# Joining, scaling and the order of the closing norms in a graph-attention kernel

## The chip, the cores and the metric

The kernel runs on one core of a Trainium2 chip. The metric is device time in microseconds (us) of one execution. TensorE, VectorE, ScalarE, GpSimd and SyncE have a queue of instructions each and run them in order; they wait for each other with semaphores. In the profile they are called PE, DVE, ACT, POOL and SP. Nearly all plain copies between memory and the on-chip SBUF are issued by SyncE.

## The reference

There are 12,500 nodes with 128 features and 412,500 edges with 64 features, sorted by target.

```python
h = node_features @ Wn + bn                      # own row of each node
hmid = leaky_relu(concat(q[src], k[tgt], eh) @ A1 + b1)
scores = leaky_relu(hmid @ A2 + b2)
w = softmax(scores.mean(axis=-1), axis=0)        # over all edges
out = segment_sum(w[:, None] * v[tgt], src, num_segments=num_nodes)
y = h + out                                      # "joined"
n = gamma * (y - mean(y)) / sqrt(var(y) + EPS) + beta   # first norm
x = layernorm(x + n)                                    # second norm
```

The softmax runs over all edges, so its denominator is known only when the last edge's score is. Until then each node's sum is kept with a reference of its own; the last step multiplies each sum by one factor and adds the own row `h`. Then come two norms over the 128 features of each node.

## The kernel before, in words

The 128 partitions hold the nodes: partition `p` holds 98 nodes in a row ("blocks" 0 to 97). A first stage (`make`) computes a record for each edge and scatters the records into tables by block. A second stage (`sums_of`) goes over 294 units (six passes over pairs of blocks) and adds weighted values to each node's sum, which is stored in the table `atab`. This second stage takes nearly all of the time. It runs a schedule written out by hand: `do(step, fn, ...)` puts a function into a numbered step, and when the program is built, the functions of one step are emitted after each other in the order in which they were put in. Each engine's queue therefore has exactly this order.

The part that is changed is `closing` (L1333 onward), which begins while the last units are still at work. It has three stages.

- Beside the second stage, `rows_x`, `moved` and `put_x` add `beta` to the node features and store them in `xtab` (GpSimd, L1354), and `load_gamma` loads `gamma` into SBUF.
- When the last unit's maximum is known, `factors`, `whole`, `spread_z`, `over_z`, `lowered_all` and `scaled_all` compute `facs`, one factor for each block (`scaled_all`, L1397, is the last).
- Then the 98 blocks are finished in 14 groups of `NB` = 7 blocks. A group is `7 x 128 = 896` numbers on each partition.

For a group the steps before the change are these. `fetch` (SyncE, L1428) loads own rows `hs`, sums `part` and moved features `xs`, each 448 KB, into one buffer of the pool `rt` (six buffers). `joined` (VectorE, L1463, seven instructions) multiplies the sum by its factor and adds the own row. `spread` (VectorE, L1440 and L1441, seven pairs) computes mean and variance of each block; `root` (ScalarE, L1444) takes the square root; `scales` (VectorE, L1447 and L1448) computes the reciprocal and an offset; `normed` (ScalarE, L1455, seven instructions) applies both. `gained` multiplies by `gamma` (VectorE, L1469) and adds `xs` (GpSimd, L1470). Then `spread`, `root`, `scales` and `normed` follow a second time, and `leave` (SyncE, L1473) writes the group to the output.

The groups overlap as a hand-written pipeline. In its step `t` the queues get, in this order: `spread` of group `t`, `gained` of group `t - 1`, the second `spread` of group `t - 2`, the first `normed` of group `t`, `joined` of group `t + 1` and the second `normed` of group `t - 2`. A group is joined in the step before its first spread, and the last group's last work is in step 15.

Of the kernel before, what the change touches and what calls it, by code (L numbers as in the profile page):

```python
# [10 lines left out]
FP = mybir.dt.float32  # L11
# [3 lines left out]
AF = mybir.ActivationFunctionType  # L15
ALU = mybir.AluOpType
# [4 lines left out]
P = 128  # L21
D = 128
# [4 lines left out]
NB = 7  # L27
# [5 lines left out]
NP = 6  # L33
CUTS = 0, 0.1266, 0.2804, 0.4615, 0.6427, 0.8238, 1
TABS = 2
WIDTH = 14
# [3 lines left out]
WR = 260  # L40
# [335 lines left out]


def first_layer(nc, banks, pk, bias):

    W = pk[:, : 4 * D].rearrange("k (s d) -> k s d", s=4)  # L380
    A1s = pk[:, 4 * D : 7 * D].rearrange("k (s d) -> k s d", s=3)
    wT = pk[:, 7 * D : 9 * D].rearrange("k (s d) -> k s d", s=2)
    weT2, cols = pk[:, 9 * D : 9 * D + 2 * DE], pk[:, 9 * D + 2 * DE : 9 * D + 2 * DE + 3]

    pw = banks[0][:, : 2 * D].rearrange("p (s d) -> p s d", s=2)
    for s in (1, 0):
        nc.tensor.matmul(pw[:, s, :], wT[:, s, :], A1s[:, s, :], start=True, stop=True)
# [60 lines left out]
def sorted_path(  # L448
# [8 lines left out]
    nc = tc.nc  # L457
# [3 lines left out]
    NBK = nb + 1  # L461
# [13 lines left out]
    ident = const.tile([P, P], FP)  # L475
# [68 lines left out]
    ng = nb // NB  # L544
# [11 lines left out]
    rp = pool("rec", 6)  # L556
    pkvp = pool("pkv", 1, space=PSUM)
    pcp = pool("pcn", 1, space=PSUM)
# [11 lines left out]
    php = pool("ph", 2, space=PSUM)  # L570
    pscp = pool("psc", 1, space=PSUM)
# [12 lines left out]
    start = const.tile([1, G], I32)  # L584
# [79 lines left out]
    with tc.tile_pool(name="prep", bufs=1) as prep:  # L664
        bank = psmp.tile([P, 4 * P], FP, name="psm")
        banks = bank[:, : 2 * D], bank[:, 2 * D :], pscp.tile([P, 4 * P], FP, name="psc")
        pk, bias = load_weights(nc, prep, pack, rows_b)
        load_first()
        W, We_, bias = first_layer(nc, banks, pk, bias)
# [6 lines left out]
        for b in range(0, NB, 2):  # L676
            m = min(2, NB - b)
            at = nodes[b // 2][:, : 2 * D * m]
            for k in range(m):
# [40 lines left out]
    def spans():  # L720
# [24 lines left out]
        out=above, in_=above, compare_op=ALU.is_gt, fill=0.0, base=0,  # L745
# [8 lines left out]
    pcs = {}  # L754
# [232 lines left out]
    for p, t in enumerate(plan.tiles):  # L987
        wide = max(1, min(2, WIDTH // t))
# [347 lines left out]
    def closing(bp, do, s0, s1, s2):  # L1336

        gb = {}

        def wide(b):  # L1340
            return b.rearrange("p (o d) -> p o d", o=1).to_broadcast([P, NB, D])

        def three(b, k):
            return b[:, k * NB * D : (k + 1) * NB * D].rearrange("p (b d) -> p b d", d=D)
# [86 lines left out]
        def spread(st, y, k):  # L1431
            if k == 1:
                own = (oldp, "old") if st["bl"].start // NB % 2 else (scp, "part")
                st["sm"] = own[0].tile([P, 2, D], FP, name=own[1])
            sm = st["sm"][:, k - 1, :]
            st["mv", k] = mv = sm[:, : 2 * NB].rearrange("p (b s) -> p b s", s=2)
            st["rstd", k], st["off", k] = sm[:, 2 * NB : 3 * NB], sm[:, 3 * NB : 4 * NB]
            for j in range(NB):
                s6 = sm[:, 4 * NB + 6 * j : 4 * NB + 6 * j + 6]
                nc.vector.bn_stats(s6, st[y][:, j, :])  # L1440
                nc.vector.bn_aggr(mv[:, j, :], s6)  # L1441

        def root(st, k):
# [6 lines left out]
                op0=ALU.mult, op1=ALU.mult,  # L1450
            )

        def normed(st, to, y, k):
            for j in range(NB):
                nc.scalar.activation(  # L1455
                    st[to][:, j, :], st[y][:, j, :], AF.Identity, bias=st["off", k][:, j : j + 1],
                    scale=st["rstd", k][:, j : j + 1],
                )

        def joined(st):  # L1460
            for j in range(NB):
                b = st["bl"].start + j
                nc.vector.scalar_tensor_tensor(  # L1463
                    st["hs"][:, j, :], st["part"][:, j, :], gb["facs"][:, b : b + 1], st["hs"][:, j, :],
                    op0=ALU.mult, op1=ALU.add,
                )

        def gained(st):
            nc.vector.tensor_mul(st["n1"], st["n1"], wide(gb["gamma"]))  # L1469
            nc.gpsimd.tensor_add(st["n1"], st["n1"], st["xs"])  # L1470

        def leave(st):
            nc.sync.dma_start(out=out[:, st["bl"], :], in_=st["o"])  # L1473
# [236 lines left out]
```

## Time and profile before

| What | Value |
|---|---|
| Median of 3 runs | 5028.19 us (5021.88 to 5036.83) |
| The profiled execution's own time | 5024.54 us |
| Its span, from the first to the last instruction | 5022.8 us |
| Busy share of the span: PE, DVE, ACT, POOL | 83%, 79%, 65%, 67% |
| Last multiplication on TensorE ends at | about 4880.7 us |
| Last norm on ScalarE ends at | about 5014.6 us |

A row of the profile's timeline has the start in us, the duration in us, the engine, the line of the kernel, the operation, its output and inputs, the shape of the output and of the first input, and how many equal instructions were merged (`x7`). In brackets stands the engine's idle time ahead of it. The groups of instructions by line have `busy us in total, mean ns of one`, then the idle time before them. A row of the table of stretches has the stretch, its length, the busy time of each engine with its number of instructions, the granted TensorE clock (1.00 is full speed), the share in which the DMA engines were busy, and GB/s.

### The profile page before, as it was taken

To read this page: it belongs to the slowest core of one execution; us is meant where nothing else is said; L and a number is where in the kernel's file an instruction comes from. 1 tells how busy PE (TensorE), PEld (TensorE's weight loads), DVE (VectorE), ACT (ScalarE), POOL (GpSimd) and SP (SyncE) were. 2 spreads that over 40 slices of the span, in tenths; PEclk is the share of its full clock that TensorE was granted. 3 is DMA by queue.
4 is the path that set the end of the run, shared out by engine and by line. 5 is a ranking of instruction groups with operands and counts; after the bars stand their busy time and mean duration, and the time that the engine had idled before them with its cause. 6 is when DMAs were issued, how large, how long until landed. Compare 5 with 4: busy or idle time off the path is not lost.

```text
span 5022.8 us, 97600 instructions
## 1 busy us (share of the span) xinstructions
PE 4158.4 (83%) x32218; PEld 3108.6 (62%) x32676; DVE 3991.7 (79%) x10036; ACT 3267.8 (65%) x8495; POOL 3348.4 (67%) x3268
## 2 busy tenths in 40 slices
PE   4565578898888888799998898999899999899980
PEld 3333356666566666577776676676667777667760
DVE  7877576788777777688888888888888888677778
ACT  3433255666566666577777777777677777677876
POOL 5777777777777777777777777777777777410002
PEclk7777588899999999899999999999999999999995
DMA  7999799998899988899989888989899999788763
GB/s 262 314 318 344 255 328 333 343 312 300 274 324 324 329 301 289 275 318 318 313 308 311 302 315 311 309 307 313 301 306 314 315 324 318 265 287 283 262 224 141
DMA packets 614992, 1505.49 MB, mean 300 GB/s; under 512 B 103587, under 2 KB 328246, under 8 KB 612681
## 3 DMA queue, kind: packets, MB, share of 16 engines
q1 hardware_dynamic: 459433, 1069.47, 65.0%
q0 software_dynamic: 154752, 429.39, 22.7%
q8 instruction: 259, 4.24, 0.3%
q14 instruction: 260, 2.13, 0.1%
q10 hardware_dynamic: 288, 0.26, 0.0%
HBM read 929.49 MB, written 608.37 MB: 306 GB/s over the span
## 4 chain that ended last, share of the span: by engine, by line
DMA 37%; PE 24%; DVE 16%; POOL 9%; issue 6%; ACT 6%; SPq 1%; DVEq 0%; ACTq 0%; POOLq 0%
DMA rtab<-rec,idx 14%; DMA rt<-rtab 13%; POOL rtab L904 9%; PE psm L1268 6%; DMA row<-slT 4%; PE ph L1116 4%; PE pkv L881 3%; PE ph L1107 3%; DMA rowB<-row 3%; DVE hm L1131 2%; PE psc L1144 2%; PE pkv L875 2%; ACT rec L892 2%; PE psm L1177 2%; ACT ohw L1239 2%
## 5 line engine op out<-in xcount | busy, mean ns | idle before, releaser
L904 POOL DMA_INDIRECT rtab<-rec,idx x3224 | 3286.2, 1019 | 1042.0 <-issue 781.0
L892 ACT ACTIVATE rec<-pkv 128x1024 f32<-128x1024 f32 x806 | 819.9, 1017 | 863.5 <-PE pkv L881 475.4
L1239 ACT ACTIVATE ohw<-ohs,w 128x128 f32<-128x128 bf16 x3822 | 1258.7, 400 | 58.4 <-DVE ohs L1225 47.9
L1268 PE MATMUL psm<-rt,ohw 128*128 128x128 f32 x7644 | 1158.6, 294 | 10.7 <-ACT ohw L1239 10.6
L1268 PEld LDWEIGHTS psm<-rt,ohw 128*128 128x128 f32 x7644 | 997.5, 200 | 59.5 <-ACT ohw L1239 17.7
L1127 ACT ACTIVATE hm<-ph 128x512 f32<-128x512 f32 (+1 forms) x1078 | 581.7, 540 | 461.6 <-PE ph L1116 429.0
L1116 PE MATMUL ph<-ohT,qs 128*128 128x512 bf16 (+3 forms) x3658 | 718.1, 312 | 25.5 <-issue 2.6
L1131 DVE TENSOR_TENSOR hm<-ph,hm 128x512 f32<-128x512 f32 (+1 forms) x1078 | 668.5, 620 | 83.3 <-ACT hm L1127 81.9
L875 PE MATMUL pkv<-kvs,ohd 128*128 128x256 bf16 x3224 | 531.4, 292 | 204.0 <-ACT rec L892 189.7
L1107 PE MATMUL ph<-ident,rt 128*128 128x128 f32 x3822 | 629.3, 283 | 45.8 <-DVE hm L1131 43.4
L881 PE MATMUL pkv<-WeS,eat 64*128 64x128 f32 x6448 | 633.6, 320 | 0.0
L1096 DVE TENSOR_SCALAR ohT<-rowB,iotaP 128x512 bf16<-128x512 uint8 (+1 forms) x1078 | 518.4, 481 | 102.1 <-DMA rowB<-row 97.2
L881 PEld LDWEIGHTS pkv<-WeS,eat 64*128 64x128 f32 x6448 | 467.9, 205 | 191.8 <-issue 184.9
L875 PEld LDWEIGHTS <-ohd 128*128 128x128 bf16 x3224 | 316.2, 103 | 317.5 <-issue 224.5
L1107 PEld LDWEIGHTS ph<-ident,rt 128*128 128x128 f32 x3822 | 471.9, 152 | 64.1 <-DVE hm L1131 51.0
L1116 PEld LDWEIGHTS <-qs 128*128 128x128 bf16 x4116 | 396.8, 100 | 129.4 <-issue 4.8
L1225 DVE TENSOR_TENSOR ohs<-iotaE,sl 128x512 bf16<-128x512 bf16 (+1 forms) x1078 | 427.1, 396 | 48.4 <-ACT ohw L1239 46.8
L844 DVE TENSOR_TENSOR ats<-pc,oh 128x792 f32<-128x792 f32 x403 | 392.1, 973 | 82.1 <-PE pc L826 76.9
L1144 PE MATMUL psc<-hm,A2s 128*32 128x512 f32 (+3 forms) x2352 | 337.7, 538 | 80.1 <-DVE slT L1075 75.9
L1177 PE MATMUL psm<-headsum,z 128*128 128x4 f32 (+1 forms) x2156 | 287.9, 255 | 128.0 <-DVE part L1284 87.0
L855 DVE TENSOR_REDUCE pos<-ats 128x8 f32<-128x792 f32 x403 | 390.2, 968 | 4.2
L1177 PEld LDWEIGHTS psm<-headsum,z 128*128 128x128 f32 (+1 forms) x2156 | 280.9, 202 | 149.4 <-DVE part L1284 102.6
(161 smaller groups left out, 4080.2 us busy)
## 6 DMA issues: line engine op xcount, KB each, us to landing
rt<-rtab SPq DMA_DIRECT2D x196, 1820.0 KB
eat<-in_ea SPq DMA_DIRECT2D x201, 512.0 KB
rt<-rtab SPq DMA_DIRECT2D x49, 1560.0 KB
rt<-rtab SPq DMA_DIRECT2D x49, 1300.0 KB
qs<-qtab SPq DMA_DIRECT2D x294, 192.0 KB
rtab<-rec,idx POOLq DMA_INDIRECT x3224
dstb<-dtab SPq DMA_DIRECT2D x201, 256.0 KB
rtab<-empty SPq DMA_DIRECT2D x98, 520.0 KB
```

Of the source, the lines that this page charges most:

```text
L875: nc.tensor.matmul(pk[:, h, i, :], ohd[:, t * P : (t + 1) * P], kvs, start=(i == 0), stop=False,)
L881: nc.tensor.matmul(pk[:, h, i, :D], eat[h * DE : (h + 1) * DE, (j + i) * P : (j + i + 1) * P], WeS[h * DE : (h + 1) * DE, :], start=False, ...
L892: nc.scalar.activation(rec[:, :, :, : 2 * D], pk, AF.Copy)
L904: one_tile = nc.gpsimd.indirect_dma_start(out=rtab[p % TABS][:, :], out_offset=bass.IndirectOffsetOnAxis(ap=idxs[g][:, t : t + 1], axis=0) ...
L1096: nc.vector.tensor_scalar(st["oh"][k][:, : n * P], st["rowB"][:, t0 * P : (t0 + n) * P], iotaP, None, op0=ALU.is_equal,)
L1107: nc.tensor.matmul(ph[:, j * P : (j + 1) * P], st["rt"][:, t0 + j, :D], ident, is_transpose=True, start=(j == 0), stop=False,)
L1116: nc.tensor.matmul(ph[:, cols], st["qs"][:, j0 // t, s, :], oh[:, cols], start=False, stop=(s == 2 and j1 == t0 + n),)
L1127: nc.scalar.activation(hm, state[i]["ph", k][:, : n * P], AF.Copy, scale=SLOPE)
L1131: nc.vector.tensor_tensor(hm, ph[:, : n * P], hm, op=ALU.max)
L1177: nc.tensor.matmul(st["psS"][:, t0 + j : t0 + j + (nv - 1) * sw + 1 : sw], z[: 32 * nv, j * P : (j + 1) * P], headsum[: 32 * nv, :nv], sta ...
L1239: nc.scalar.activation(ohw[:, j, :], ohs[:, :, j], AF.Copy, scale=st["w"][:, t0 + j : t0 + j + 1])
L1268: nc.tensor.matmul(st["psS"][:, (1 + u) * P : (2 + u) * P], ohw[:, j, :], st["rt"][:, t0 + j, D : 2 * D], start=(k == 0), stop=(k == t - 1),)
```

## The change

Nothing outside `closing` does other work; the tile `pc` of the first stage is only allocated at the width of the others (512 numbers instead of 99), so that `closing` can use its buffer. In `closing`:

- `diagonals` is new: GpSimd multiplies the identity matrix by the factors of four pairs of blocks, which gives four 128 x 128 diagonal matrices (two neighbouring blocks share one, because they come from one unit and have the same factor).
- `joined` moves to TensorE: two multiplications by the identity bring the own rows into PSUM (512 and 384 columns), and seven multiplications by a diagonal add the scaled sums. Three sets of PSUM buffers are used in turn: `pkv`; two `ph`; `psc` and `pc`.
- The first `spread` and the first `normed` read PSUM; `normed` writes its result into a buffer of the pool `rec`, and the second norm is written in place and leaves from there.
- `gained` multiplies by `gamma` on GpSimd instead of VectorE.
- A group takes one step more, and the order within a step is another. `scales` of both norms stand in the middle of a `spread` of another group.

```diff
     def begin(p):
-        pcs[p] = pcp.tile([P, NBK], FP, name="pc")
+        pcs[p] = pcp.tile([P, 4 * P], FP, name="pc")[:, :NBK]
...
-            st["n1"], st["o"] = three(rt, 3), st["part"]
+        pairs = max(1, min(2, WIDTH // plan.tiles[NP - 1]))
+        def diagonals(st):
+            b0, b1 = st["bl"].start // pairs * pairs, st["bl"].stop
+            n = -(-(b1 - b0) // pairs)
+            rec = rp.tile([P, 2, 2, WR], FP, name="rec").rearrange("p a b w -> p (a b w)")
+            dg = rec[:, : n * P].rearrange("p (n d) -> p n d", n=n)
+            nc.gpsimd.tensor_tensor(
+                dg, ident.rearrange("p (o d) -> p o d", o=1).to_broadcast([P, n, P]),
+                gb["facs"][:, b0:b1:pairs].rearrange("p (n o) -> p n o", o=1)
+                .to_broadcast([P, n, P]),
+                op=ALU.mult,
+            )
+            st["dg"] = lambda b: dg[:, (b - b0) // pairs, :]
+        def joined(st):
+            g = st["bl"].start // NB
+            if g % 3 == 0:
+                pk = pkvp.tile([P, 2, 2, 2 * D], FP, name="pkv").rearrange("p h i w -> p h (i w)")
+                st["y"] = pk[:, 0, :], pk[:, 1, :]
+            elif g % 3 == 1:
+                st["y"] = [php.tile([P, 4 * P], FP, name="ph") for _ in range(2)]
+            else:
+                st["y"] = (
+                    pscp.tile([P, 4 * P], FP, name="psc"), pcp.tile([P, 4 * P], FP, name="pc")
+                )
+            for k, to in enumerate(st["y"]):
+                m = min(4, NB - 4 * k)
+                nc.tensor.matmul(
+                    to[:, : m * P], ident,
+                    st["hs"][:, 4 * k : 4 * k + m, :].rearrange("p b d -> p (b d)"),
+                    start=True, stop=False,
+                )
+                for j in range(m):
+                    nc.tensor.matmul(
+                        to[:, j * P : (j + 1) * P], st["dg"](st["bl"].start + 4 * k + j),
+                        st["part"][:, 4 * k + j, :], start=False, stop=(j == m - 1),
+                    )
...
-        def joined(st):
-            for j in range(NB):
-                b = st["bl"].start + j
-                nc.vector.scalar_tensor_tensor(
-                    st["hs"][:, j, :], st["part"][:, j, :], gb["facs"][:, b : b + 1], st["hs"][:, j, :],
-                    op0=ALU.mult, op1=ALU.add,
-                )
...
         def gained(st):
-            nc.vector.tensor_mul(st["n1"], st["n1"], wide(gb["gamma"]))
+            nc.gpsimd.tensor_mul(st["n1"], st["n1"], wide(gb["gamma"]))
             nc.gpsimd.tensor_add(st["n1"], st["n1"], st["xs"])
...
-        for t in range(-1, ng + 2):
+        for t in range(-4, ng + 3):
             s = first + t
-            at(s - 3, t + 1, fetch)
-            at(s, t, spread, "hs", 1)
-            at(s, t, root, 1)
-            at(s, t - 1, gained)
-            at(s, t - 2, spread, "n1", 2)
-            at(s, t - 2, root, 2)
-            at(s, t, scales, 1)
-            at(s, t, normed, "n1", "hs", 1)
-            at(s, t + 1, joined)
-            at(s, t - 2, scales, 2)
-            at(s, t - 2, normed, "o", "n1", 2)
-            at(s, t - 2, leave)
+            at(s, t + 4, fetch)
+            at(s, t + 2, diagonals)
+            at(s, t + 1, joined)
+            at(s, t - 1, normed, 1)
+            at(s, t, spread, 1, 0, 3)
+            at(s, t - 3, scales, 2)
+            at(s, t, spread, 1, 3, NB)
+            at(s, t, root, 1)
+            at(s, t - 3, normed, 2)
+            at(s, t - 3, leave)
+            at(s, t - 2, spread, 2, 0, 4)
+            at(s, t, scales, 1)
+            at(s, t - 2, spread, 2, 4, NB)
+            at(s, t - 2, root, 2)
+            at(s, t - 1, gained)
```

In the changed kernel the lines are: diagonals L1437, joined L1458 and L1464, spread L1483 and L1484, root L1487, scales L1490 and L1491, normed L1501, gained L1507 and L1508, leave L1511.

More of the change, by code (lines that the diff above doesn't have):

```diff
@@ L1428, in fetch, with of, spread @@
                 nc.sync.dma_start(out=st[name], in_=of[:, bl, :])
-            st["n1"], st["o"] = three(rt, 3), st["part"]
-        def spread(st, y, k):
+        pairs = max(1, min(2, WIDTH // plan.tiles[NP - 1]))
[34 more added lines that the diff above has]
+                    )
+        def of(st, k, j):
             if k == 1:
+                return st["y"][j // 4][:, j % 4 * P : (j % 4 + 1) * P]
+            return st["n1"][:, j, :]
+        def spread(st, k, j0, j1):
+            if k == 1 and j0 == 0:
                 own = (oldp, "old") if st["bl"].start // NB % 2 else (scp, "part")
@@ L1437, in spread @@
             st["rstd", k], st["off", k] = sm[:, 2 * NB : 3 * NB], sm[:, 3 * NB : 4 * NB]
-            for j in range(NB):
+            for j in range(j0, j1):
                 s6 = sm[:, 4 * NB + 6 * j : 4 * NB + 6 * j + 6]
-                nc.vector.bn_stats(s6, st[y][:, j, :])
+                nc.vector.bn_stats(s6, of(st, k, j))
                 nc.vector.bn_aggr(mv[:, j, :], s6)
@@ L1451, in scales, with normed @@
             )
-        def normed(st, to, y, k):
+        def normed(st, k):
+            if k == 1:
+                rec = rp.tile([P, 2, 2, WR], FP, name="rec").rearrange("p a b w -> p (a b w)")
+                st["n1"] = three(rec, 0)
             for j in range(NB):
                 nc.scalar.activation(
-                    st[to][:, j, :], st[y][:, j, :], AF.Identity, bias=st["off", k][:, j : j + 1],
-                    scale=st["rstd", k][:, j : j + 1],
-                )
-        def joined(st):
-            for j in range(NB):
-                b = st["bl"].start + j
-                nc.vector.scalar_tensor_tensor(
-                    st["hs"][:, j, :], st["part"][:, j, :], gb["facs"][:, b : b + 1], st["hs"][:, j, :],
-                    op0=ALU.mult, op1=ALU.add,
+                    st["n1"][:, j, :], of(st, k, j), AF.Identity,
+                    bias=st["off", k][:, j : j + 1], scale=st["rstd", k][:, j : j + 1],
                 )
         def gained(st):
-            nc.vector.tensor_mul(st["n1"], st["n1"], wide(gb["gamma"]))
+            nc.gpsimd.tensor_mul(st["n1"], st["n1"], wide(gb["gamma"]))
             nc.gpsimd.tensor_add(st["n1"], st["n1"], st["xs"])
         def leave(st):
-            nc.sync.dma_start(out=out[:, st["bl"], :], in_=st["o"])
+            nc.sync.dma_start(out=out[:, st["bl"], :], in_=st["n1"])
         groups = [dict(bl=slice(g * NB, (g + 1) * NB)) for g in range(ng)]
```

## The prediction

> **What bounds the kernel now.** I first read the table of stretches of the last 320 us, because only the closing changes: the queues keep their order up to the first diagonal.
>
> ```profile
> 4700.00:4862.00 162.00, 159.85 (x1229) 123.05 (x1245) 124.58 (x358) 132.01 (x390) 0.00 (x0) 1.00 0.69 232
> 4904.00:4994.00 90.00, 0.00 (x0) 0.00 (x0) 84.47 (x400) 59.17 (x160) 20.72 (x10) 0.50 0.48 175
> ```
>
> Up to 4862 PE is busy all the time. From 4904 to 4994 PE does nothing, DVE is busy for 84 of 90 us, ACT for 59, POOL for 21. The rest of the kernel can't gain; what is to be had lies here. Next, one period of the pipeline in the timeline of DVE, then the rows of ACT and POOL beside it:
>
> ```profile
> 4937.40 1.93 DVE L1463 SCALAR_TENSOR_TENSOR rt<-rt,hm 128x128 f32<-128x128 f32 x7
> 4939.25 0.19 DVE L1447 RECIPROCAL part<-part 128x7 f32<-128x7 f32 x1
> ...
> 4939.56 0.29 DVE L1440 BATCH_NORM_STATS2 old<-rt 128x6 f32<-128x128 f32 x1
> ...
> 4942.34 1.06 DVE L1469 TENSOR_TENSOR rt<-rt,eat 128x896 f32<-128x896 f32 x1
> 4943.32 0.29 DVE L1440 BATCH_NORM_STATS2 old<-rt 128x6 f32<-128x128 f32 x1
> ...
> 4946.10 0.17 DVE L1447 RECIPROCAL old<-old 128x7 f32<-128x7 f32 x1
> 4946.31 0.17 DVE L1448 SCALAR_TENSOR_TENSOR old<-old 128x7 f32<-128x7 f32 x1
> 4946.42 1.93 DVE L1463 SCALAR_TENSOR_TENSOR rt<-rt,hm 128x128 f32<-128x128 f32 x7
> ```
>
> ```profile
> 4937.20 0.30 ACT L1444 ACTIVATE part<-part,eps 128x7 f32<-128x7 f32 x1 [3.00 <-DVE part L1441]
> 4937.49 5.49 ACT L1455 ACTIVATE rt<-rt,part 128x128 f32<-128x128 f32 x14
> 4943.53 2.07 POOL L1470 TENSOR_TENSOR rt<-rt 128x896 f32<-128x896 f32 x1 [6.95 <-DVE rt L1469]
> ```
>
> DVE has no gap, so the period is the sum of its parts, from start to start: join 1.85, scales 0.31, spread 2.78, gamma 0.98, spread 2.78, scales 0.32: 9.02 us. ACT needs 5.49 + 2 x 0.29 = 6.07 and waits 3 us.
>
> **The change part by part.** Joins and gamma leave DVE: 9.02 - 1.85 - 0.98 = 6.19 us a step are left. That is the gain if nothing else ends later; so I ask of each other engine what its step becomes.
>
> ACT keeps its 14 norms and two roots, 6.07 us by the rows above; seven norms now read PSUM. The nearest rows:
>
> ```profile
> L1455 ACT ACTIVATE rt<-rt,part 128x128 f32<-128x128 f32 x98 | 38.5, 479 | 1.0 <-DVE part L1448 1.0
> L1159 ACT ACTIVATE z<-psc,b_c 96x512 f32<-96x512 f32 x8 | 5.3, 669 | 0.0
> L1159 ACT ACTIVATE z<-psc,b_c 32x256 f32<-32x256 f32 x8 | 3.7, 466 | 0.2
> ```
>
> The same function from PSUM costs 0.79 ns an element (203 ns for 256 elements more), so 0.365 us at 128 against 0.479 from SBUF. Seven take 2.74 us at the old spacing of 0.392, and 2.0 if all of that difference comes off the spacing. I keep both ends.
>
> The first spread reads PSUM. No row has it; L1284, with PSUM for one of its inputs, and L1463, with SBUF alone, cost the same:
>
> ```profile
> L1284 DVE SCALAR_TENSOR_TENSOR part<-old,by,psm 128x128 f32<-128x128 f32 x20 | 5.9, 338 | 0.0
> L1463 DVE SCALAR_TENSOR_TENSOR rt<-rt,hm 128x128 f32<-128x128 f32 x98 | 26.9, 345 | 0.0
> ```
>
> I take no difference; 0.05 us an instruction either way would be 0.35 a step.
>
> PE gets 896 identity and 896 diagonal columns a group. Warm and cold rows:
>
> ```profile
> 4650.90 0.89 PE psm L1268 x8
> 39.12 2.07 PE L1534 MATMUL ph<-hm,xt 128*128 128x256 f32 x4 [8.98 <-DMA xt<-in_xN]
> 25.00:50.00 25.00, 11.21 (x58) 7.45 (x59) 14.09 (x35) 3.94 (x6) 7.20 (x8) 0.63 0.76 220
> ```
>
> Eight records are four f32 multiplications of 128 columns (two records each): 0.22 us each at full clock, so 14 x 0.22 = 3.1 us a group. At the low clock two of 256 columns took 2.07: 14 x 0.52 = 7.2 us. A group can be joined as soon as the norm three groups earlier has read its PSUM, over a step before it is needed, so either fits in a step of 7.2 us or more. PE's price lies in the start, below. If its cover goes (a step below 7.2 with a cold PE), PE sets 7.2.
>
> The Trainium skill ("TensorE: Matmul & The Clock Gate", Part 1) says that the clock is halved by default and is released by some 3.4 us of sustained matmuls. The stretch with the clock at 0.63 and PE half busy agrees; by this rule the joins, bursts of 3 to 7 us, would run between the two prices, and the sum stays within mine.
>
> POOL gets a multiplication of 896 (L1354, an addition with a broadcast input, is the nearest) and the diagonals, 512 numbers:
>
> ```profile
> L1354 POOL TENSOR_TENSOR rec<-rec x14: 2085/2094/2272, 4366.8 to 4584.8; 128x896 f32<-128x896 f32 x14
> ```
>
> 2.09 for gamma, 2.07 for the addition; for the diagonals 512/896 x 2.07 = 1.18, with something fixed 1.25 (bounds: 1.2 and 2.1, a full row). Together 5.4 us with gaps of 0.1: below 6.19, but POOL is now nearly always busy. What that does to DVE is the crux:
>
> ```profile
> 4890.20 2.07 POOL L1470 TENSOR_TENSOR rt<-rt 128x896 f32<-128x896 f32 x1 [303.29 <-DVE old L1447]
> 4890.22 2.08 DVE L1448 SCALAR_TENSOR_TENSOR old<-old 128x7 f32<-128x7 f32 x1
> 4435.87 2.08 POOL L1354 TENSOR_TENSOR rec<-rec 128x896 f32<-128x896 f32 x1 [13.35 <-DMA rec<-in_beta]
> 4436.12 2.12 DVE L1096 TENSOR_SCALAR ohT<-rowB,iotaP 128x512 bf16<-128x512 uint8 x1
> 4943.74 0.26 DVE L1440 BATCH_NORM_STATS2 old<-rt 128x6 f32<-128x128 f32 x1
> ```
>
> The offset instruction of scales (0.17 us elsewhere) took 2.08 and ended with POOL's addition, which had begun 0.02 before. So did L1096, which reads one tensor: 2.12 us, to the end of the addition of 4435.87. Spreads are not held up (the one at 4943.74 runs within the POOL addition of 4943.53). Scales has one offset instruction, and there are two scales a step. Of its reciprocal (one tensor) no row tells; I take it to run like the spreads, and the other case is a rival.
>
> The Trainium skill ("SBUF — State Buffer", "Who interferes with whom") has this rule: a DVE instruction with two SBUF inputs and a GpSimd instruction that reads SBUF exclude each other, and the later one waits for the whole of the other. The trace agrees, with 2.08 us for the offset's two inputs. By the rule the reciprocal, with one, doesn't wait, and the sum is the one below; if it waited, that of rival 2.
>
> The steady step by hand, us from the start of DVE's step: ACT's last root ends at 0.32; the first norm runs until 3.06; POOL multiplies 3.19 to 5.28, adds 5.38 to 7.45, makes diagonals 7.55 to 8.80. DVE reaches the first norm's offset after three pairs of a spread (0.393 each), the other scales, four pairs, four pairs of the other spread and the reciprocal, 1.18 + 0.31 + 1.57 + 1.57 + 0.22 = 4.85: it waits until 5.28, and with 0.09 + 1.18 after it the step is 6.55. In the next step the diagonals run until 8.80 - 6.55 = 2.25, and the second norm's offset, due at 1.40, waits 0.85; the first's comes at 5.70, in the addition, and waits until 7.45: a step of 8.72. After that the diagonals are over by 0.08, and 6.55 follows. So the steps alternate, 7.64 on average. With norms from PSUM at 2.0 us, POOL multiplies 2.45 to 4.54 and adds until 6.71; each 4.85 falls into the addition: 7.98 every time. Between them (norms of 2.3 us) 6.11 and 8.28 alternate: 7.2. I take 7.8.
>
> The start and the end of the pipeline:
>
> ```profile
> 4878.32 0.27 DVE L1397 TENSOR_SCALAR hm<-hm,rs 128x98 f32<-128x98 f32 x1
> 4880.48 0.28 DVE L1440 BATCH_NORM_STATS2 part<-rt 128x6 f32<-128x128 f32 x1
> ...
> 4903.55 0.29 DVE L1440 BATCH_NORM_STATS2 old<-rt 128x6 f32<-128x128 f32 x1
> ...
> 4993.69 0.28 DVE L1440 BATCH_NORM_STATS2 old<-rt 128x6 f32<-128x128 f32 x1
> 5007.72 0.20 DVE L1447 RECIPROCAL part<-part 128x7 f32<-128x7 f32 x1 [0.37 <-ACT part L1444]
> 5011.76 2.80 ACT L1455 ACTIVATE rt<-rt,old 128x128 f32<-128x128 f32 x7 [0.52 <-DVE old L1448]
> ```
>
> Before, group 0's spread starts at 4880.48, group 3's at 4903.55, group 13's at 4993.69 (ten steps of 9.01), and the last norm ends at 5014.56. After: factors ready 4878.6; diagonals until 4880.0; four diagonal multiplications, the second identity and three more, 0.9 + 0.67 + 0.67, until 4882.3: spread 0 is 1.9 late. Spread, root (DVE waits 0.37 for it at 5007.72) and scales take 3.4: spread 1 at 4885.9. The norm of group 0 (2.74) lets POOL multiply from 4888.8 to 4890.9, and the offset of group 1 waits for it: spread 2 at 4891.0; likewise for the next multiplication, which ends at 4896.6: spread 3 at 4897.9. That is 5.6 earlier than before; with a cold PE some 4 us of it go. The ten steps: 10 x (9.01 - 7.8) = 12.1. The end, from group 13's spread: a step of 7.8, then root 0.3, norm 2.74, POOL 4.3, spread 2.8, root and scales 0.7, norm 2.74: 21.4 against 20.87, a loss of 0.5. With 1 us for a partly cold PE in the start: 5.6 - 1 + 12.1 - 0.5 = 16 to 17; with 7.64 for the step it is 18. I forecast 17 us less.
>
> What I cost at nothing: the SyncE queue. A group's 4 copies of 448 KB in 7.8 us are 235 GB/s:
>
> ```profile
> out<-rt SPq DMA_DIRECT2D x14, 448.0 KB
> ```
>
> ```profile
> 4880.00:4890.00 10.00, 0.67 (x6) 0.48 (x5) 9.08 (x44) 4.79 (x11) 0.00 (x0) 0.69 1.03 411
> ```
>
> 411 are shown. Fetches stand in the same steps as before; `leave`, now one step later, waits for the later norm with the next fetch behind it, three steps before that data is needed. A buffer `rt` is now free after POOL's addition instead of after the output's copy. In the built order four `rec` buffers take turns for the norms, so a norm waits for the copy issued a full step earlier; if that cover went, each us beyond a step would be paid. The wider `pc` moves nothing in the first stage.
>
> **The rivals.**
>
> 1. The port costs little (offsets fall between POOL's operations, as would be with other phases): DVE's 6.1 to 6.6 a step, 24 to 29 less in the steps and 4 at the ends: 28 to 33 us less. Against it: POOL is busy for 5.4 us of them. 0.12.
> 2. The port costs more: the reciprocal waits too, or POOL's next operation takes the port ahead of the waiting offset. No row has a reciprocal beside POOL. With the reciprocal: it waits out the multiplication, the offset the addition, 8.0 to 8.72 each step: 3 to 10 less in the steps and about none at the ends. Losing the port twice: until 8.80, so 10.07 a step: 10.5 more, less 3 from the ends. In all 10 us less to 8 more. 0.18.
> 3. Slower: POOL becomes the bound. No row shows a POOL multiplication, nor an input that repeats one number along the run, as the factors do in the diagonals. The step must reach (15 + 4)/10 + 9.01 = 10.9 to lose 0.3%, so these two 10.9 - 2.07 - 0.3 = 8.5 us, against 3.3 taken. 0.08.
>
> **How the numbers follow.** The profiled execution, 5024.54 us, lies 3.65 under the median of 5028.19. From the median: 5028 - 17 = 5011. The likeliest case has 0.62; its own range follows from 7.2 to 8.1 a step and a warm or cold PE in the start: 10 to 23 less, 5005 to 5018. Rival 1 gives 4995 to 5000, rival 2 5018 to 5036, rival 3 over 5043. From 4994 to 5027 rival 3 and half of rival 2 are left out, under 2 in 10. A measurement can tell 0.3%, 15 us (the three runs spread by as much). Faster by more: rival 1 and three quarters of the likeliest, 0.58. Within: the rest of it and rival 2, 0.34. Slower: rival 3, 0.08.
>
> **What would show it.** Right: from 4900 on a step of 7 to 8 us between the first spreads; some offset instructions (L1491) of 0.5 to 2 us that end with a POOL operation; POOL busy for two thirds; ACT no longer waiting for DVE alone. Wrong: offsets of 0.17 throughout, diagonals or gamma over 3 us, PE waited for by spreads in each step, reciprocals of over 1 us, or a norm that waits for an output copy.

## The result and the profile after

The changed kernel takes 5005.80 us (median of 8 runs, 4995.99 to 5014.24), the kernel before beside it 5025.32 us (8 runs). The medians differ by 19.5 us (a ratio of 0.9961); the ratio on record, 0.9954 with a 95% interval of 0.9945 to 0.9963, is not that of the two medians and gives 23 us: faster by about 0.4 to 0.5%. The prediction said 5011 us, and 17 us less. The profiled execution has a time of its own of 5003.96 us and a span of 5001.9 us.

A measure recurs below: the "closing", from the start of the instruction that makes the factors (L1397) to the end of the last norm on ScalarE. It was 136.24 us before (4878.32 to 5014.56) and is 113.13 now, 23.1 less; the front of the kernel was 2.1 us later in this execution.

The stretches after the change, in the same view as before (PE, PEld, DVE, ACT, POOL busy; then the clock, the DMA share and GB/s):

```profile
4700.00:4862.00 162.00, 160.93 (x1249) 122.46 (x1248) 124.82 (x360) 133.55 (x395) 0.00 (x0) 1.00 0.69 240
4900.00:4975.00 75.00, 40.19 (x166) 28.71 (x164) 69.29 (x335) 58.66 (x165) 52.66 (x30) 0.78 0.56 200
```

The front is as it was. In the pipeline VectorE is still nearly always busy (69.3 of 75 us), and GpSimd is now busy for 70%. Part of VectorE's busy time is waiting, as its offset instructions (L1491) over two steps of the pipeline show, beside GpSimd's rows in the timeline:

```profile
4931.53 0.61 DVE L1491 SCALAR_TENSOR_TENSOR part<-part 128x7 f32<-128x7 f32 x1
...
4935.25 0.17 DVE L1490 RECIPROCAL old<-old 128x7 f32<-128x7 f32 x1
4935.45 1.87 DVE L1491 SCALAR_TENSOR_TENSOR old<-old 128x7 f32<-128x7 f32 x1
...
4939.86 0.17 DVE L1491 SCALAR_TENSOR_TENSOR old<-old 128x7 f32<-128x7 f32 x1
...
4943.35 0.17 DVE L1491 SCALAR_TENSOR_TENSOR part<-part 128x7 f32<-128x7 f32 x1
```

```profile
4926.88 2.08 POOL L1507 TENSOR_TENSOR rec<-rec,eat 128x896 f32<-128x896 f32 x1 [3.08 <-ACT rec L1501]
...
4931.08 1.04 POOL L1437 TENSOR_TENSOR rec<-ident,hm 128x512 f32<-128x512 f32 x1
4933.06 2.08 POOL L1507 TENSOR_TENSOR rec<-rec,eat 128x896 f32<-128x896 f32 x1 [0.95 <-ACT rec L1501]
4935.22 2.08 POOL L1508 TENSOR_TENSOR rec<-rec,rt 128x896 f32<-128x896 f32 x1
...
4941.38 2.08 POOL L1507 TENSOR_TENSOR rec<-rec,eat 128x896 f32<-128x896 f32 x1 [3.08 <-ACT rec L1501]
```

The offset of 4931.53 begins within the diagonals (L1437, 4931.08 to 4932.12) and ends with them, 0.61 us later. That of 4935.45 begins within the addition (L1508, 4935.22 to 4937.30) and ends with it, 1.87 us later. The reciprocal at 4935.25 stands within the same addition and takes its usual 0.17. In the next step both offsets take their usual 0.17: that of 4939.86 stands outside GpSimd's instructions, and that of 4943.35 begins only 0.11 us before the multiplication of 4941.38 ends (4943.46), too late for a wait to show. The multiplications (L1507) start at 4926.88, 4933.06 and 4941.38: steps of 6.2 and 8.3 us in turn.

The norms of ScalarE, first from PSUM and then from SBUF, in its timeline, and below them the groups of instructions (busy in total, mean ns of one, idle time before them):

```profile
4930.45 2.53 ACT L1501 ACTIVATE rec<-pkv,part 128x128 f32<-128x128 f32 x7
...
4934.00 2.79 ACT L1501 ACTIVATE rec<-rec,part 128x128 f32<-128x128 f32 x7
```

```profile
L1507 POOL TENSOR_TENSOR rec<-rec,eat 128x896 f32<-128x896 f32 x14 | 29.1, 2080 | 32.8 <-ACT rec L1501 25.1 <-PE pc L1458 7.7
L1501 ACT ACTIVATE rec<-rec,old 128x128 f32<-128x128 f32 x49 | 19.5, 483 | 0.6 <-DVE old L1491 0.6
L1437 POOL TENSOR_TENSOR rec<-ident,hm 128x512 f32<-128x512 f32 x14 | 14.5, 1042 | 290.6 <-DVE hm L1397 290.6
L1458 PE MATMUL pkv<-rt,ident 128*128 128x512 f32 x10 | 8.3, 924 | 11.6 <-ACT rec L1501 11.6
L1483 DVE BATCH_NORM_STATS2 part<-pkv 128x6 f32<-128x128 f32 x21 | 5.7, 270 | 5.4 <-PE pkv L1464 5.4
```

Seven norms from PSUM take 2.53 us; gamma on GpSimd takes 2.08, the diagonals 1.04. TensorE waits for a norm to free its PSUM (11.6 us), and the spreads wait for TensorE only once, at the start (5.4 us). The start and the end of the pipeline in VectorE's and ScalarE's timeline:

```profile
4880.43 0.27 DVE L1397 TENSOR_SCALAR hm<-hm,rs 128x98 f32<-128x98 f32 x1
4886.12 0.30 DVE L1483 BATCH_NORM_STATS2 part<-pkv 128x6 f32<-128x128 f32 x1 [5.42 <-PE pkv L1464]
...
4901.58 0.29 DVE L1483 BATCH_NORM_STATS2 old<-pkv 128x6 f32<-128x128 f32 x1
...
4973.64 0.27 DVE L1483 BATCH_NORM_STATS2 old<-ph 128x6 f32<-128x128 f32 x1
```

```profile
4990.76 2.80 ACT L1501 ACTIVATE rec<-rec,old 128x128 f32<-128x128 f32 x7 [0.55 <-DVE old L1491]
```

The rows are those of groups 0, 3 and 13, and the last norm. From L1397 on, group 3 starts 21.15 us later (25.23 before), the ten steps to group 13 take 72.06 (90.14 before), and from there it is 19.92 to the end of the last norm (20.87 before): 4.1, 18.1 and 0.9 us less, 23.1 in all.

### The profile page after: what moved, and what is told of

It is laid out like the page before. It is cut to its first block, busy times and chain, and to the rows that moved or that the text cites. A ratio compares the mean times of both kernels' runs of the same rounds, so it can differ in the third digit from the quotient of the medians.

```text
span 5001.9 us, 98498 instructions
## 1 busy us (share of the span) xinstructions
PE 4244.8 (85%) x32928; PEld 3144.3 (63%) x32928; DVE 3969.5 (79%) x9924; ACT 3262.3 (65%) x8495; POOL 3398.0 (68%) x3296
## 4 chain that ended last, share of the span: by engine, by line
DMA 34%; PE 23%; DVE 17%; POOL 11%; issue 7%; ACT 7%; SPq 1%; ACTq 0%; DVEq 0%; POOLq 0%
DMA rtab<-rec,idx 15%; DMA rt<-rtab 11%; POOL rtab L904 11%; PE psm L1268 6%; PE ph L1116 4%; PE ph L1107 3%; DMA row<-slT 3%; PE pkv L881 3%; DVE hm L1131 2%; ACT rec L892 2%; PE psc L1144 2%; DMA rowB<-row 2%; PE pkv L875 2%; ACT ohw L1239 2%; PE psm L1177 2%
## 5 line engine op out<-in xcount | busy, mean ns | idle before, releaser
L1268 PE MATMUL psm<-rt,ohw 128*128 128x128 f32 x7644 | 1157.2, 294 | 11.8 <-ACT ohw L1239 11.6
L1116 PE MATMUL ph<-ohT,qs 128*128 128x256 bf16 (+3 forms) x4116 | 817.2, 320 | 0.0
L1096 DVE TENSOR_SCALAR ohT<-rowB,iotaP 128x512 bf16<-128x512 uint8 (+1 forms) x1078 | 518.7, 481 | 84.7 <-DMA rowB<-row 80.0
```

The source lines that it names most:

```text
L1096: nc.vector.tensor_scalar(st["oh"][k][:, : n * P], st["rowB"][:, t0 * P : (t0 + n) * P], iotaP, None, op0=ALU.is_equal,)
L1116: nc.tensor.matmul(ph[:, cols], st["qs"][:, j0 // t, s, :], oh[:, cols], start=False, stop=(s == 2 and j1 == t0 + n),)
L1268: nc.tensor.matmul(st["psS"][:, (1 + u) * P : (2 + u) * P], ohw[:, j, :], st["rt"][:, t0 + j, D : 2 * D], start=(k == 0), stop=(k == t - 1),)
```

## The experiments

The theory: VectorE's own work sets the step (9.0 us before, 6.2 after), and to it come the waits of those VectorE instructions that read two tensors from SBUF and fall into an instruction of GpSimd. The rivals: GpSimd's own work sets the step; all of VectorE's work beside GpSimd is slower; the new order of four steps brings the gain. The kernels x1 to x4 ran on a chip on which the kernel before takes 6132.56 us (25 runs, clock 0.84), x5 to x8 on one where it takes 5034.89 (12 runs), x9 to x11 on one with 5036.80 (17 runs). The closing of each comes from one profiled execution. The closings are what is compared across chips: single instructions of the closing take the same time on the slow one (GpSimd's addition 2.07 us, an offset 0.17).

| Kernel | Median us | Ratio to before, interval | Closing us | Step us |
|---|---|---|---|---|
| before | 5025.32 | | 136.24 | 9.02 |
| changed kernel | 5005.80 | 0.9954, 0.9945 to 0.9963 | 113.13 | 6.2 and 8.3 |
| x1_gamma | 6122.79 | 0.9987, 0.9972 to 1.0003 | 123.58 | 8.02 |
| x2_join | 6111.62 | 0.9967, 0.9952 to 0.9982 | 122.58 | 7.90 |
| x3_psum | 6095.76 | 0.9944, 0.9925 to 0.9963 | 103.48 | 6.18 |
| x4_twice | 6109.48 | 0.9954, 0.9938 to 0.9970 | 114.58 | 6.33 and 8.33 |
| x5_thrice | 5018.57 | 0.9967, 0.9956 to 0.9979 | 117.74 | 7.44 |
| x6_order | 5052.56 | 1.0040, 1.0026 to 1.0054 | 156.66 | 10.8 |
| x7_psum | 5004.70 | 0.9938, 0.9925 to 0.9951 | 103.43 | 6.18 |
| x8_after | 5007.71 | 0.9956, 0.9942 to 0.9971 | 111.55 | 6.2 and 8.3 |
| x9_moved | 5032.09 | 0.9992, 0.9983 to 1.0001 | 135.12 | 8.99 |
| x10_psum | 5002.13 | 0.9932, 0.9919 to 0.9945 | 103.44 | 6.18 |
| x11_after | 5010.67 | 0.9946, 0.9933 to 0.9959 | 111.57 | 6.2 and 8.3 |

**Gamma alone.** The kernel before, with one edit:

```diff
-            nc.vector.tensor_mul(st["n1"], st["n1"], wide(gb["gamma"]))
+            nc.gpsimd.tensor_mul(st["n1"], st["n1"], wide(gb["gamma"]))
```

> The kernel before, with one part of the change: GpSimd multiplies by gamma; joins and order stay. Theory (VectorE bounds each step, and only an offset instruction of scales that falls into a GpSimd operation is held up): VectorE's step loses the 0.98 us of the multiplication, 9.02 to 8.04; GpSimd multiplies and adds from about 0.7 to 5.0 of a step, and both offsets, at 5.8 and 7.9, fall behind that, so they stay at 0.17 us. Ten steps give 9.8 us and the ends 2 to 4: 12 to 14 us less than before (ratio 0.9973). Rival (GpSimd's work holds VectorE up wherever it stands): offsets or joins of 1 to 2 us in each step, steps of 9 us or more, no gain.

Two steps of its pipeline, GpSimd's multiplications in the timeline:

```profile
6032.32 2.08 POOL L1469 TENSOR_TENSOR rt<-rt,eat 128x896 f32<-128x896 f32 x1 [3.75 <-ACT rt L1455]
...
6040.34 2.08 POOL L1469 TENSOR_TENSOR rt<-rt,eat 128x896 f32<-128x896 f32 x1 [3.80 <-ACT rt L1455]
```

The step is 8.02 us: 9.02 less the 0.98 of gamma. The offsets take 0.17 in the steady steps, because they stand outside GpSimd's two instructions here. The closing falls by 12.7 us, 9.6 of it in the ten steps from group 3 to group 13. In the whole time of 6.1 ms it is hardly to be told from nothing.

**Order and joins, gamma left on VectorE.** The changed kernel, with this edit:

```diff
-            nc.gpsimd.tensor_mul(st["n1"], st["n1"], wide(gb["gamma"]))
+            nc.vector.tensor_mul(st["n1"], st["n1"], wide(gb["gamma"]))
```

> The changed kernel with the multiplication by gamma put back on VectorE: joins on TensorE and the order of four steps remain. Theory: VectorE's own work is 6.2 + 0.98 = 7.2 us a step; GpSimd adds at the start of the next step, and the second norm's offset, due at 1.4, waits about 0.8 us for it: 7.9 to 8.0 a step, 11 to 14 us less than before (ratio 0.9975). Rival (no wait for the port): 7.2 a step, 20 us less, as much as the whole change.

```profile
6046.05 0.17 DVE L1491 SCALAR_TENSOR_TENSOR old<-old 128x7 f32<-128x7 f32 x1
...
6049.74 0.88 DVE L1491 SCALAR_TENSOR_TENSOR old<-old 128x7 f32<-128x7 f32 x1
```

```profile
6040.63 2.07 POOL L1508 TENSOR_TENSOR rec<-rec,rt 128x896 f32<-128x896 f32 x1 [4.82 <-ACT part L1487]
...
6048.53 2.07 POOL L1508 TENSOR_TENSOR rec<-rec,rt 128x896 f32<-128x896 f32 x1 [4.82 <-PE pkv L1464]
```

The step is 7.90: 9.02 less the join's 1.85, and 0.7 for one offset that falls into the addition (0.88 instead of 0.17) and ends with it at 6050.6. GpSimd idles 4.8 us of each step, so it isn't GpSimd's own work that sets it. The whole time, 20 us less by the ratio with an interval of 11 to 29, can't tell the expected 11 to 14 from the rival's 20; the step can.

**Mean and variance in PSUM.** The changed kernel; the offset instruction then has one input in PSUM and one in SBUF. The same work otherwise:

```diff
-            st["mv", k] = mv = sm[:, : 2 * NB].rearrange("p (b s) -> p b s", s=2)
+            if j0 == 0:
+                mean = sm if st["bl"].start < 4 * NB else psmp.tile([P, 4 * P], FP, name="psm")
+                st["mv", k] = mean[:, : 2 * NB].rearrange("p (b s) -> p b s", s=2)
+            mv = st["mv", k]
```

> The changed kernel with mean and variance of groups 4 to 13 written to PSUM, so that the offset instruction reads one tensor of SBUF and one of PSUM; nothing else. Theory (the two-tensor read of SBUF is what waits for GpSimd): all offsets from group 4 on take 0.17 us, and VectorE runs through: 6.2 to 6.3 us a step instead of 7.25 on average, about 10 us less than the changed kernel, 32 us less than before (ratio 0.9935). Rival (the chain from ScalarE's norm over GpSimd's two operations sets the step, and the waits only fill time that VectorE has to spare): steps stay at 7.2, ratio as the changed kernel's 0.9954.

GpSimd's timeline, one offset in VectorE's, and the view of the offset's line (ns: least, median, most; start of the first and the last):

```profile
6033.31 2.08 POOL L1511 TENSOR_TENSOR rec<-rec,rt 128x896 f32<-128x896 f32 x1
...
6050.19 2.09 POOL L1510 TENSOR_TENSOR rec<-rec,eat 128x896 f32<-128x896 f32 x1 [0.92 <-ACT rec L1504]
6052.36 2.07 POOL L1511 TENSOR_TENSOR rec<-rec,rt 128x896 f32<-128x896 f32 x1
...
6056.38 2.09 POOL L1510 TENSOR_TENSOR rec<-rec,eat 128x896 f32<-128x896 f32 x1 [0.94 <-ACT rec L1504]
```

```profile
6033.56 0.17 DVE L1494 SCALAR_TENSOR_TENSOR old<-psm,old 128x7 f32<-128x7 f32 x1
```

```profile
L1494 DVE SCALAR_TENSOR_TENSOR old<-psm,old x10: 165/166/167, 6033.6 to 6094.9; 128x7 f32<-128x7 f32 x10
L1494 DVE SCALAR_TENSOR_TENSOR old<-old x4: 167/666/1806, 6006.1 to 6036.3; 128x7 f32<-128x7 f32 x4
```

All offsets with the mean in PSUM take 0.165 to 0.167 us, though GpSimd does the same work as in the changed kernel; those of the first groups, with the mean in SBUF, took up to 1.81. The offset of 6033.56 begins 1.83 us before the addition of 6033.31 ends, where one in the changed kernel took 1.87, and takes 0.17. Once the means are in PSUM, every step but one (6.7) is 6.2 us, VectorE's own work. That shows the cause of the steps of 8.3, and that ScalarE and GpSimd can follow a step of 6.2. The closing is 103.5 us, 9.7 less than in the first profiled execution of the changed kernel and 8.1 less than in the two later ones (x8, x11 below).

**The same diagonals twice, and three times.** After the instruction that makes them, the same instruction stands once more (x4) or twice more (x5):

```diff
+            nc.gpsimd.tensor_tensor(
+                dg, ident.rearrange("p (o d) -> p o d", o=1).to_broadcast([P, n, P]),
...
+                op=ALU.mult,
+            )
```

> The changed kernel with each group's diagonals computed twice (the same result), 1.04 us more of GpSimd work a step. Theory: the length of a pair of steps is set by the multiplication and the addition that the first norm's offset waits out, not by the diagonals: steps go on alternating at 6.2 and 8.3, only the start is some 1 to 2 us later; the second norm's wait of 0.6 grows to about 1.7, and the first norm's wait of 1.9 shrinks by as much. Within 3 us of the changed kernel (ratio 0.9954 to 0.9961). Rival (GpSimd's total work sets the pace): 1 us more a step, 10 to 14 us more than the changed kernel (ratio 0.998).

```profile
6031.92 2.09 POOL L1513 TENSOR_TENSOR rec<-rec,eat 128x896 f32<-128x896 f32 x1 [1.96 <-ACT rec L1507]
...
6038.25 2.08 POOL L1513 TENSOR_TENSOR rec<-rec,eat 128x896 f32<-128x896 f32 x1
...
6046.57 2.08 POOL L1513 TENSOR_TENSOR rec<-rec,eat 128x896 f32<-128x896 f32 x1 [1.96 <-ACT rec L1507]
```

The pair of steps is 14.65 us against 14.5: 1.04 us more of GpSimd's work in each step costs 0.08 of it. (The closing is 3.0 us longer than in x8 and x11: 2.3 of that come before group 3, where the first spread alone waits 1.04 for the added instruction, and 0.8 in the ten steps.) The short step is now the sum of GpSimd's instructions with no idle time, the long one has 1.96 us to spare.

> The changed kernel with GpSimd making the same diagonals three times: 2.1 us more on GpSimd in each step than in the changed kernel, to the same result. My theory (an offset instruction of VectorE waits for the GpSimd instruction it falls into, and nothing else of GpSimd counts): the third instruction now reaches into the other offset's place in the short step too, so that no step is short any more: 8.3 to 8.5 us each instead of 6.2 and 8.3 in turn, offsets of 0.6 to 2 us in every step. The closing, 113 us from the factors to the last norm in the changed kernel, becomes 122 to 127 (twice cost only 1.5). Ratio to the kernel before 0.997 to 0.998. Rival (GpSimd's own work sets the step, which is now 2.08 + 2.08 + 3 x 1.04 and gaps, 7.5 us): steps of 7.5, a closing of 116 to 117. Rival (each added us is paid): 2.1 more than the changed kernel per step, 9.3, a closing of 134 or more, no gain left.

GpSimd's and VectorE's timeline with three:

```profile
4930.33 2.08 POOL L1519 TENSOR_TENSOR rec<-rec,eat 128x896 f32<-128x896 f32 x1
4932.49 2.08 POOL L1520 TENSOR_TENSOR rec<-rec,rt 128x896 f32<-128x896 f32 x1
4934.52 1.04 POOL L1437 TENSOR_TENSOR rec<-ident,hm 128x512 f32<-128x512 f32 x1
4935.65 1.04 POOL L1443 TENSOR_TENSOR rec<-ident,hm 128x512 f32<-128x512 f32 x1
...
4937.77 2.09 POOL L1519 TENSOR_TENSOR rec<-rec,eat 128x896 f32<-128x896 f32 x1
```

```profile
4931.47 0.97 DVE L1503 SCALAR_TENSOR_TENSOR old<-old 128x7 f32<-128x7 f32 x1
...
4934.97 0.62 DVE L1503 SCALAR_TENSOR_TENSOR old<-old 128x7 f32<-128x7 f32 x1
```

My expectation fell: the step is 7.44 us, not 8.3 to 8.5, and the rival named it (7.5). GpSimd has no idle time left and is now the bound. My error was to walk through the three as one block of 3.1 us. They are three instructions, and a waiting offset gets in when the current one ends: that of 4934.97 ends at 4935.59, with the first of the three (4935.56), though the second was next in GpSimd's queue. So the wait is never longer than the rest of one instruction. The closing is 6.2 us longer than that of the changed kernel on the same chip (x8). Of this 3.4 is the start: the first spread comes 7.51 us after L1397 instead of 4.11, behind two more instructions for the diagonals and then a slower TensorE (granted clock 0.50 from 4892 to 4894). The rest is mostly steps of 7.44 instead of 7.2 on average.

**The order alone.** The changed kernel with joins and gamma back on VectorE, and no diagonals (`joined`, not shown, is that of the kernel before, and the first spread and norm read its result in SBUF):

```diff
...
-            nc.gpsimd.tensor_mul(st["n1"], st["n1"], wide(gb["gamma"]))
+            nc.vector.tensor_mul(st["n1"], st["n1"], wide(gb["gamma"]))
...
-            at(s, t + 2, diagonals)
```

> The four-step order of the changed kernel alone: the joins are on VectorE again, in SBUF, the multiplication by gamma too, and there are no diagonals; outputs leave from the normed buffer as in the changed kernel. My theory (VectorE's own work sets the step wherever no offset falls into GpSimd's addition): 9.0 us a step as before, offsets of 0.17, a closing of 135 to 139 us against 136.2 in the kernel before, ratio 0.9995 to 1.0005: the order brings nothing by itself. Rival (the kernel before lost time to the order, by waits between VectorE and ScalarE in each step): a step under 8.8 and a ratio under 0.9985.

The view of the joins' line, and one step in VectorE's and GpSimd's timeline:

```profile
L1448 DVE SCALAR_TENSOR_TENSOR rt<-rt,hm x14: 338/342/2167, 4951.4 to 4965.6; 128x128 f32<-128x128 f32 x14
```

```profile
4962.21 3.74 DVE L1448 SCALAR_TENSOR_TENSOR rt<-rt,hm 128x128 f32<-128x128 f32 x7
...
4962.51 2.24 POOL L1492 TENSOR_TENSOR rec<-rec,rt 128x896 f32<-128x896 f32 x1 [8.56 <-ACT rec L1485]
...
4973.31 2.24 POOL L1492 TENSOR_TENSOR rec<-rec,rt 128x896 f32<-128x896 f32 x1 [8.56 <-ACT rec L1485]
```

Neither theory nor rival: the order alone is slower, by 0.4%, with a step of 10.8 us. The offsets are free (median 0.17), but the joins now stand right behind gamma, where the addition starts, and they too read two tensors from SBUF: one of seven takes 2.17 us and ends 0.15 after the addition. 9.0 + 1.8 is 10.8. I had applied my own rule to the offsets only.

**The order alone, the join moved.** Of x6, within a step:

```diff
-            at(s, t + 1, joined)
             at(s, t - 1, normed, 1)
             at(s, t, spread, 1, 0, 3)
-            at(s, t - 3, scales, 2)
             at(s, t, spread, 1, 3, NB)
             at(s, t, root, 1)
+            at(s, t - 3, scales, 2)
+            at(s, t + 1, joined)
```

> The four-step order alone once more (joins and gamma on VectorE, no diagonals), with two things moved within a step: the whole first spread comes first, and the later scales and the join stand behind it. In the order alone the join stood right behind gamma, where GpSimd's addition starts, and one of its seven instructions took 2.17 us instead of 0.34; the step was 10.8. My theory now (every VectorE instruction with two inputs from SBUF waits for a GpSimd instruction under way, the joins too): the join, now 3 us after the addition starts, isn't held up, each of its instructions takes 0.34, the step is 9.0 and the closing 136 to 140 us, ratio 0.999 to 1.001. Rival (the order costs by something else, such as waits on ScalarE): a step of 10 us or more and a ratio over 1.002.

```profile
L1448 DVE SCALAR_TENSOR_TENSOR rt<-rt,hm x98: 331/346/353, 4884.1 to 4992.4; 128x128 f32<-128x128 f32 x98
```

```profile
4952.06 2.08 POOL L1492 TENSOR_TENSOR rec<-rec,rt 128x896 f32<-128x896 f32 x1 [6.90 <-DVE part L1467]
...
4961.05 2.08 POOL L1492 TENSOR_TENSOR rec<-rec,rt 128x896 f32<-128x896 f32 x1 [6.92 <-DVE old L1467]
```

As the theory says: all 98 joins take 0.33 to 0.35 us and the step is 8.99; the closing of 135.1 is 1 us below what I expected. Where an instruction with two SBUF inputs stands within the step is worth 1.8 us a step, 18 of the 21.5 us between this closing and that of x6; 1.8 more is the start, where in x6 two groups are joined ahead of the first spread. With the join moved the new order alone leaves the closing within 1.1 us of that before, so by itself it brings next to nothing. Joins on TensorE in the old order were not run; what the order adds to them stays open.

**The changed kernel and the one with means in PSUM, side by side, two times.** The first has no edit, the second is x3's.

> The changed kernel itself, unaltered, beside the others on one chip. My theory: 0.995 to 0.997 of the kernel before, the closing about 113 us, steps of 6.2 and 8.3 in turn; the first spread 4 us after the factors if the clock holds, 5.7 if it drops as in the first execution.

> Once more the changed kernel with mean and variance of groups 4 to 13 in PSUM, on the chip of the changed kernel's own timed run beside it. My theory (the offset instruction with two inputs from SBUF is what waits for GpSimd): steps of 6.2 throughout instead of 6.2 and 8.3 in turn, 9 to 11 us less than the changed kernel, ratio to the kernel before 0.992 to 0.995 by the chip's clock. Rival (the steps of 8.3 come from ScalarE or GpSimd): as the changed kernel.

> The changed kernel itself, unaltered, as the measure for the one with mean and variance in PSUM: 0.995 to 0.996 of the kernel before.

> The changed kernel with mean and variance of groups 4 to 13 in PSUM, again beside the changed kernel: the whole time, in which the two couldn't be told apart before. Expected from the closings (103.4 and 111.6 us): 8 us less than the changed kernel, ratio to the kernel before 0.993 to 0.995. Rival (the gain is given back behind the last norm or hidden by the front): as the changed kernel, within 3 us.

The closings repeat within 0.1 us: 111.6 and 103.4. In the whole time the version with means in PSUM is 3.0 us ahead in the first comparison, less than the 9 to 11 that I expected there, and 8.5 in the second. The intervals of the ratios overlap, so that whole times alone would not settle it; the closing's 8.1 us do. It is the fastest of all kernels tried, 0.9932 and 0.9938 of the kernel before.

## Why the prediction was right

**The number.** It is closer than the sum behind it. The closing, which the prediction walked through, is 23.1 us shorter (24.7 in x8 and x11), against a sum of 16 to 17 and a likeliest range of 10 to 23. The first comparison's medians differ by 19.5 us, those of x8 and x11 by 27.2 and 26.1 (by the ratios on record 23, 22 and 27). That the first medians lie near 17 is partly luck: the front varies by more than that (the factors come at 4880.4, 4880.9 and 4889.0 in the three profiled executions of the changed kernel). The direction and the mechanism were right; what the sum made too small is the gain of the steps.

**The bound and the gain.** Right: VectorE's step set the end, and 9.02 - 1.85 - 0.98 = 6.19 is what is left of its own work. x3 shows 6.18 once nothing waits; x1 shows gamma's part alone, and x2 the join's, with one wait of 0.7 on top.

**The waits on GpSimd.** Right, in detail: the offset waits to the end of the GpSimd instruction it falls into, the reciprocal (0.17 to 0.20 us in all 28) and the spreads don't. Rival 2's first half, a reciprocal that waits, is ruled out by the row at 4935.25, its second, GpSimd ahead of a waiting offset, by x5. The Trainium skill ("SBUF — State Buffer", "Who interferes with whom") says that a VectorE instruction contends with GpSimd's reads when it has two SBUF inputs and, outside its 2-port modes, doesn't with one. The closings of all runs here agree; the clearest number is x3's 0.167 us at most, with one of the two inputs moved to PSUM. The prediction's L1096, which reads one tensor and was held up for 2.12 us, would by this be in such a mode; no run here shows whether it is.

**The step's size.** This is the mis-sized term. The prediction took 7.8 us out of three cases and so 12.1 us for the ten steps; they are 7.2 on average and gave 18.1. The alternation that it walked through came. Its sizes were off in two places. Seven norms take 2.53 us, not 2.74 or 2.0: with 2.53 the same walk gives 6.34 and 8.51, 7.4 on average, and the case of 2.0 us, whose 7.98 had pulled the choice from 7.64 up to 7.8, didn't occur. The other 0.2 lies where one engine takes over from another: the multiplication starts 0.08 us after the norm (4932.98 to 4933.06) instead of 0.13, an offset that falls into its last 0.1 us isn't held up, and the spread behind a held offset starts 0.06 before the addition ends (4937.24 and 4937.30) instead of 0.09 after it. The diagonals, 1.04 instead of 1.25, change nothing: with either the walk gives the same steps, and in x4 twice the diagonals cost 0.08 a step. That the measured 6.2 and 8.3 are nearly those of the case with norms of 2.3 (6.11 and 8.28, mean 7.2) comes of the two together. The walk jumps between patterns, so a mean of its cases is none of them.

**Start and end.** Predicted 4.6 less and 0.5 more, measured 4.1 less and 0.9 less. In the start of the profiled execution the first spread is 3.5 us late instead of 1.9 (5.69 us after L1397, 2.16 before). TensorE had waited 1.1 us for `zp`, and behind that the clock in the rows is low:

```profile
4882.00:4884.00 2.00, 2.00 (x5) 1.01 (x6) 0.00 (x0) 1.47 (x2) 2.00 (x3) 0.58 1.03 417
```

```profile
4881.89 1.99 PE L1458 MATMUL pkv<-rt,ident 128*128 128x512 f32 x2
```

In x8, the same kernel, the clock is 1.00 there:

```profile
4882.00:4884.00 2.00, 2.00 (x12) 1.46 (x11) 0.00 (x0) 1.93 (x4) 2.00 (x3) 1.00 1.05 422
```

```profile
4881.62 1.13 PE L1458 MATMUL pkv<-rt,ident 128*128 128x512 f32 x2
...
4884.99 0.30 DVE L1483 BATCH_NORM_STATS2 part<-pkv 128x6 f32<-128x128 f32 x1 [3.84 <-PE pkv L1464]
```

There the spread comes 4.11 us after L1397, 1.95 late, as predicted for a warm TensorE, and the start's gain is 5.65 (5.6 predicted, though its single steps are off by up to 0.5 us, which cancel). So the 1 us taken off for a partly cold TensorE is the difference between executions, 1.6 us. The Trainium skill ("TensorE: Matmul & The Clock Gate", Part 1) says that activity is measured in a window that runs freely, so that the number of slow multiplications at a kernel's start varies between runs of one kernel; these two executions, though at the kernel's end, agree in that the outcome varies, with 0.58 and 1.00. It puts the return to the low clock behind an idle window of some 3.4 us; the longest gap in the 10 us ahead of the drop was 1.1 us, so in that the trace differs. Why the clock fell in the one execution and not in the other stays open. The end is better because group 13's own step is a short one, 6.2 instead of 7.8.

**What was costed at nothing.** Right: the norms' idle time is all VectorE's offsets, not copies; the spreads wait for TensorE only in the start; in the view of waits no engine waits for a DMA between 4884 and the last instruction. First spreads from PSUM take 270 ns against 264.

**Rivals 1 and 3.** Rival 1's 28 to 33 us less would need free offsets; x3 frees them and its closing is 32.8 us shorter than before. Rival 3, GpSimd as the bound, needs more than it has: in x5 it becomes so at 7.44, and the kernel is still faster than before.

## What to carry to other kernels

When work moves to GpSimd, list every VectorE instruction with two SBUF inputs and ask which GpSimd instruction it falls into: each costs up to the rest of that instruction, and moving it within the step, or putting one input into PSUM, takes the cost away. Walk at least three steps by hand, because the waits shift the phase and the steps can alternate; report the cases and don't average them. A change of 20 us in 5000 shows far more clearly in the stage that it touches, here the time from the factors to the last norm, than in the whole time.

## What the runs showed of the hardware that was not expected

- A multiplication of 896 float32 numbers on GpSimd takes what an addition takes (2.08 us), also with a broadcast input, as the prediction assumed without a row for it; 512 numbers with both inputs broadcast take 1.04.
- ScalarE's norm of 128 columns takes 452 to 461 ns from `pkv`, `ph` and `psc` in PSUM, 475 from `pc`, and 478 to 483 from SBUF; seven in a row take 2.53 from `pkv` and 2.79 from SBUF: the estimate from L1159 (365 ns) was too low.
- In x6 GpSimd's addition takes 2.24 us, where a join is under way when it begins (a join runs from 4962.47 to 4962.82, the addition begins at 4962.51), instead of the 2.08 that it takes in x9. That the one causes the other is not shown.
- A waiting VectorE instruction gets in between two GpSimd instructions even where GpSimd has its next one ready (x5: an offset ends at 4935.59, between GpSimd's end at 4935.56 and its next start at 4935.65).
- An offset that begins in the last 0.1 to 0.15 us of a GpSimd instruction shows no wait (0.17 us at 4943.35).
